# Attention with a low-rank expert layer on one core: one product tile of the first pair is moved between the two halves of block 1's values, and block 0's gates are transposed one item later

## Chip, cores and metric

One Trainium2 chip, one of its cores. The metric is the device time of one execution in microseconds (us). The kernel before was run four times: 2584.33, 2585.94, 2585.36 and 2582.39 us, median 2584.85 us.

## The reference, cut to what matters

Two sequences of 2048 rows with 2048 features each are normalised; the result feeds a single-head attention of width 512 and a low-rank expert layer with a router. Both are added to the input.

```python
xn = _layernorm(x)
x = x + attn(xn, Wqkv, bqkv, Wo, bo) + ffn(xn, A_w, B_w, Wq_w, keys)
# attn: q, k, v = xn @ Wqkv + bqkv;  softmax(q k^T / sqrt(512)) v;  @ Wo + bo
# ffn:
q      = xn @ Wq_w.T                  # 16 router features of a row
scores = q @ keys.T                   # 64 experts
gate   = softmax over the 16 largest scores, 0 elsewhere
z      = xn @ A_w.T                   # 64 experts x 8
out    = (z * gate) @ B_w.T * 2
```

Everything is float32. All products are made from a high part and a low part of each operand, so each product of two 128-wide pieces is three matmuls.

## The kernel before, in words

**Blocks and pairs.** The 4096 rows are cut into blocks of 512 rows; two blocks make a pair. The first stage (up to 1296 us) makes queries, keys, gated features and values of all blocks. The later stages (scores, softmax, weighting, output product) are not touched by the change. A pair's product is computed with seven block products in place of eight (`PHASES`: P1, P2, P6, P5, P3, P7, P4), from sums and differences of the four quarters of the input (`xq` tiles) and of the weights. The first pair is special. Its block 0 is made in the plain way (`first_block`, L319 and on, then `features`, L866), and for block 1 the values are made in two halves of the input's features, called Q and R (`values_by_half`, L902).

**Units of work ("items").** An item is what one or two loaded weight pieces feed:

- `features()`: 12 items k = 0 to 11. Each has 8 products, that is 24 matmuls with 512 columns.
- `values_by_half()`: phases Q and R, for each h = 0, 1 and g = 0, 1. One (phase, h, g) is 48 matmuls with 264 columns. The four row tiles t of one h accumulate in four PSUM banks over g = 0 and 1.
- `third()` (L948): the six P3 tiles in the order `MIXED` = 0, 2, 4, 1, 3, 5. Each is 24 matmuls with 512 columns; ScalarE copies the result into a `wu` tile (L964).
- Then `phase(0, "P6")`, P5, P7 and P4, each with six items of 24 matmuls.

**Weight pieces.** The list `pieces` (L588) fixes the order in which pieces are loaded. At the end of each item `fetch(n + 1)` (L602) issues the load of the piece two items ahead on SyncE's DMA queue (L621), casts it on ScalarE to its high part (`split_hi`, L127) and subtracts on VectorE for its low part (`split_lo`, L130). The raw tiles `pw` have three slots and the split tiles six (three pieces).

**PSUM.** `acc()` hands out seven banks in rotation. In Q and R each h takes four of them. So the last of the four tiles of (R, 1) gets the bank of the first tile of (R, 0), and a matmul into it has to wait until that tile has been read out.

**What leaves R.** `values_half_out` (L931) first adds the 16 router columns of each of the four tiles into `qr1` (L942), then calls `values_out` (L291 and on) for each: VectorE adds the Q half (L302), ScalarE casts the high part (L127), VectorE makes the low part (L130), and `store`/`flush` (L170) sends the tile to `v_d`. The tile `vs` has two slots (`mid(0, 1)`), so the third tile's add needs the first tile's store to have landed.

**Side work, dealt by hand.** `beside_F` and `beside_V` say what is recorded after which item. For the stretch in question this is: `L[n]`, `S_[n]`, `O[n]` (`part_load`, `part_sums`, `part_out`, L1160 to L1175): loads of weight quarters, four sums on GpSimd (`four_sums`, L537, lines 540 to 543) and the stores of the results to `sq_d`, from which later pieces are loaded; `b1` (`whole`, L1137) and `t2` (L666): sums on VectorE that later phases need; `p6`: splits of `t` tiles for P6; `st`: row statistics of block 2 (loads of `xs` on ScalarE's queue, L243, and `bn_stats` on VectorE, L225); and the router of block 1: `router(qr1)` (a transposition, L463), `choose` (L468: scores, the 16 largest, softmax, result `wk`), and later `gates` (L497: transposition of `wk`, L500, copy, four stores to `gd`).

**What sets the order.** A list scheduler orders the instructions of each engine before the run; `behind(...)` tells it to place a step behind some instruction already recorded. At run time every engine and every DMA queue works strictly in that order, and waits on semaphores.

**Block 0's gates.** In `features()`, after item 0 comes `router`, after item 1 `choose`, after item 3 `gates(0, wk)` (L896). The two gate tiles are loaded (`gate`, L513) at items 8 and 9, and first used on VectorE at the end of item 10 (L531).

Of the kernel before, what the change touches and what calls it, by code (L numbers as in the profile page):

```python
# [62 lines left out]
def attn_ffn_kernel(ctx: ExitStack, tc, x, xT, wq, wv, wob, bqk, bv, bo, keysT, out):  # L63
# [17 lines left out]
    def big(*js):  # L81
        return Ring(sb, *(f"B{j}" for j in js))
# [17 lines left out]
    def acc(n=None):  # L100

        if n is None:
            n = banks.pop(0)
            banks.append(n)
        return psum.tile([P, T], F32, name="acc", tag=f"acc{n}", bufs=1)

    def misc(shape=None):
        return psum.tile(shape or [P, T], F32, name="misc", tag="misc", bufs=1)
# [352 lines left out]
    def router(qr):  # L461
        pt = misc([P, P])
        nc.tensor.transpose(pt, qr.rearrange("p t r -> p (t r)"), ident)  # L463
        qT = r_qT([P, P], F32, "qT")
        nc.scalar.copy(qT, pt)
        return qT

    def choose(qT):  # L468
        psc = misc([P, NT, NE])
        nc.tensor.matmul(  # L470
            psc.rearrange("p t e -> p (t e)"), qT, kblk.rearrange("p t e -> p (t e)"),
            start=True, stop=True,
        )
        sc = r_sc([P, NT, NE], F32, "sc")
        nc.scalar.copy(sc, psc)
        wk = r_wk([P, NT, NE], F32, "wk")
        m8 = const.tile([P, NT, 2, 8], F32, name="m8")
        for t in range(NT):
            nc.vector.max(m8[:, t, 0, :], sc[:, t, :])
            nc.vector.match_replace(wk[:, t, :], m8[:, t, 0, :], sc[:, t, :], LOW)  # L480
            nc.vector.max(m8[:, t, 1, :], wk[:, t, :])
            nc.vector.match_replace(wk[:, t, :], m8[:, t, 1, :], wk[:, t, :], LOW)
        nc.vector.tensor_tensor(
            sc, sc, m8[:, :, 0, 0:1].to_broadcast([P, NT, NE]), ALU.subtract
        )
        nc.scalar.activation(sc, sc, AF.Exp)
        nc.vector.scalar_tensor_tensor(wk, wk, LOW, sc, ALU.is_equal, ALU.mult)
        sm = const.tile([P, NT], F32, name="sm")
        nc.vector.tensor_reduce(sm, wk, AX.X, ALU.add)
        nc.vector.reciprocal(sm, sm)  # L490
        nc.vector.tensor_scalar(sm, sm, 2.0, None, ALU.mult)
        nc.vector.tensor_tensor(
            wk, wk, sm.unsqueeze(2).to_broadcast([P, NT, NE]), ALU.mult
        )
        return wk
# [17 lines left out]
    def gate(gf, n):  # L513
        g = r_g([P, T], F32, "g")
        nc.sync.dma_start(g, gf[n * P : (n + 1) * P, :])
        return g
# [37 lines left out]
    def value_sums(m):  # L554
# [32 lines left out]
    MIXED = (0, 2, 4, 1, 3, 5)  # L587
    pieces = [  # L588
        (0, "F", 2 * p + f1, ch) for p in range(NFP // 2) for ch in range(2) for f1 in range(2)
    ]  # L590
    pieces += [(0, ph, h, g) for ph in "QR" for h in range(2) for g in range(2)]
    pieces += [(0, "P3", it, 0) for it in MIXED]
    pieces += [(0, ph, it, 0) for ph in ("P6", "P5", "P7", "P4") for it in range(NFP)]
    pieces += [
        (j, ph, it, g)
# [270 lines left out]
    def features():  # L866


        tiles, qT, wk, gx = {}, None, None, {}
        for k, (_, _, fp, ch) in enumerate(pieces[:12]):  # L870
            if ch == 0:
                tiles[fp] = acc()
            ps, w = tiles[fp], ready.pop(k)
            if fp >= 2 * 2 and ch == 0:
                gx[fp - 4] = gate(gfs[0], fp - 4)
            for c in range(HC):
                product(
                    ps, lambda a: w[a][:, c * P : (c + 1) * P], lambda b: xn[ch * HC + c][b],
                    c == 0 and ch == 0, c == HC - 1, ch == 1,
                )  # L880
            last["dve1"] = last["dve"]
            fetch(k + 2)
            flush()
            if ch == 0:
                if fp % 2 == 0:
                    XU[0, fp // 2] = r_xu([P, 2, T], F32, "xu")
                nc.scalar.copy(XU[0, fp // 2][:, fp % 2, :], ps)
            else:
                feature_out(0, ND * (fp // 2) + fp % 2, ps, gx)
            with behind("pe"):  # L890
                if k == 0:
                    qT = router(qr)
                if k == 1:
                    wk = choose(qT)
                if k == 3:
                    gfs[0] = gates(0, wk)  # L896
            with behind("sp", "pe", "dve1"):
                for st in beside_F.get(k, []):
                    st()
        return len(tiles) * 2  # L900

    def values_by_half(n):  # L902

        for ph in "QR":
            tiles = [tsp[0, ph, 0], tsp[0, ph, 1]]
            for h in range(2):
                ps = [acc() for t in range(NT)]
                for g in range(2):
                    w = ready.pop(n)
                    n += 1  # L910
                    for cc in range(HC // 2):
                        c = g * HC // 2 + cc
                        x_ = tsp[0, ph, c // 2]
                        for t in range(NT):
                            sl = slice(t * P, (t + 1) * P)
                            product(
                                ps[t][:, :VH], lambda a: x_[a][:, c % 2, sl],
                                lambda b: w[b][:, cc, :], c == 0, c == HC - 1,
                            )
                    last["dve1"] = last["dve"]  # L920
                    fetch(n + 1)
                    if g == 1:
                        flush()
                        values_half_out(ph, h, ps)
                        flush()
                    with behind("sp", "pe", "dve1"):
                        for st in beside_V.get((ph, h, g), []):
                            st()
        return n

    def values_half_out(ph, h, ps):  # L931
# [13 lines left out]
                u = XV[0][:, t, :] if h == 0 else YV[0][t // 2][:, t % 2, :]  # L945
                values_out(1, t, h, r_vs, qr1, ps[t][:, :VH], u)

    def third(n):  # L948

        r_w = big(25), big(27), big(28)  # L950
        for m, it in enumerate(MIXED):
            ps, w = acc(), ready.pop(n)
            n += 1
            for c in range(HC):
                product(
                    ps, lambda a: w[a][:, c * P : (c + 1) * P],
                    lambda b: tsp[0, "R", c // 2][b][:, c % 2, :], c == 0, c == HC - 1,
                )
            last["dve1"] = last["dve"]
            fetch(n + 1)  # L960
            flush()
            if it % 2 == 0:
                WU[it // 2] = r_w[it // 2]([P, 2, T], F32, "wu")
            nc.scalar.copy(WU[it // 2][:, it % 2, :], ps)  # L964
            with behind("sp", "pe", "dve1"):
                for st in beside_V.get(m, []):
                    st()
        return n
# [17 lines left out]
    for k in range(NKS - 1):  # L986
        g = seq.index((k, "P3"))
# [184 lines left out]
    def part_out(n):  # L1172
# [4 lines left out]
    L, S_, O = ([lambda n=n, f=f: f(n) for n in range(8)] for f in (part_load, part_sums, part_out))  # L1177
    x01, x11 = x_steps(0, 0, 1), x_steps(0, 1, 1)
    b0, b1 = raw_steps(0), raw_steps(1)
# [3 lines left out]
    t2 = sum_steps(0, nc.vector, (0, 0), (0, 0), (0, 1), ALU.add)  # L1183
    p6 = split_steps(0, "P6", 0, 0)
# [15 lines left out]
    qr1 = None  # L1200
    state = {}
# [3 lines left out]
        ("Q", 1, 0): [O[2], L[4]] + t3[2:],  # L1205
        ("Q", 1, 1): [S_[4], L[5]] + r_[:2],
        ("R", 0, 0): [O[3], S_[5]] + r_[2:],
        ("R", 0, 1): [O[4], L[6]],
        ("R", 1, 0): [O[5], L[7], S_[6], lambda: state.update(q=router(qr1))] + b1[:2],
        ("R", 1, 1): [S_[7]] + b1[2:],  # L1210
        0: [O[6], lambda: state.update(w=choose(state["q"]))] + t2[:2],
        1: [O[7]] + p6[:1] + t2[2:],
        2: p6[1:2] + st[:2],
        3: st[2:4],
        4: p6[2:] + st[4:6],
# [1 line left out]
    }  # L1217
    r_ev = big(27, 28)
    n = features()
    qr1 = const.tile([P, NT, 32], F32, name="qr1", bufs=1)  # L1220
    nc.gpsimd.memset(qr1, 0.0)
    n = values_by_half(n)
    r_t = big(*T_SLOTS[4:], *T_SLOTS[:4])
    n = third(n)
    r_ev = big(27, 28, 29, 9)
    (la, sa, oa), (lb, sb_, ob), (lc, sc_, oc), (ld, sd_, od) = (value_sums(m) for m in range(4))
    one = lambda: gfs.update({1: gates(1, state["w"])})
    n = phase(0, "P6", n, {0: [la], 1: [sa, one], 3: [oa], 4: [lb]})
    n = phase(0, "P5", n, {0: [sb_], 2: [ob], 3: [lc]})
    n = phase(0, "P7", n, {0: [sc_], 2: [oc], 3: [ld]})  # L1230
    n = phase(0, "P4", n, {0: [sd_], 2: [od]})
    for j in PAIRS[1:]:
        for ph in PHASES:
# [5 lines left out]
            n = phase(j, ph, n)  # L1239
# [19 lines left out]
    S, tag_of, mbc, pt_, M, L, av, rl_, vt_, lsum = {}, {}, {}, {}, {}, {}, {}, {}, {}, {}  # L1259
# [224 lines left out]
    tw, S_, U, xo, bo_bc = {}, {}, {}, {}, {}  # L1484
# [228 lines left out]
    for j in range(1, NPAIR):  # L1713
# [3 lines left out]
        for n in range(7):  # L1717
            g = NG1 * j - (14, 7, 5, 4, 3, 2, 1)[n]
            if j > 1:
                deal(g, [loads[n], splits[n]], (5, 3)[n > 0])  # L1720
            else:
                g = (44, 49, 51, 52, 53, 54, 55)[n]
# [10 lines left out]
    for g in range(begin[-1]):  # L1733
# [6 lines left out]
        j, n = divmod(g, NG1)  # L1740
# [38 lines left out]
    while done < NW * NPAIR:  # L1779
# [3 lines left out]
        if d == 0 and 1 <= c <= 18:  # L1783

            k, part = (c - 1) // 2, (c - 1) % 2
# [13 lines left out]
    for q in range(2 * NG):  # L1799
# [4 lines left out]
        for n, step in enumerate(STEPS):  # L1804
# [17 lines left out]
            while at and at[0] <= n + 7 * q - 7 * (NG - 1):  # L1822
                at.pop(0)
                k = 14 - len(at)
# [47 lines left out]
```

## Time and profile before

| | us |
|---|---|
| median of 4 runs | 2584.85 |
| lowest and highest | 2582.39, 2585.94 |
| the profiled execution's own time | 2584.33 |
| its span, first to last instruction | 2582.5 |
| TensorE busy in the span | 2556.9 |
| VectorE, ScalarE, GpSimd busy | 1973.7, 927.7, 556.1 |

The profiled execution lies 0.52 us below the median of the runs, and 1.83 us of its time lie outside the span.

The stretch that the change touches runs from about 94 us (item 3 of `features()`) to about 262 us (the start of P5). Three windows of it give this table (busy us of each engine, DMA as the mean busy share of the DMA engines):

| window (us) | what runs | TensorE | VectorE | ScalarE | GpSimd | DMA |
|---|---|---|---|---|---|---|
| 94 to 140 | features, items 4 to 11 | 44.13 of 46 | 40.30 | 16.32 | 19.68 | 0.88 |
| 140 to 194 | Q and R | 49.47 of 54 | 49.88 | 16.81 | 46.56 | 0.85 |
| 194 to 262 | P3 and P6 | 68.00 of 68 | 53.44 | 28.51 | 15.35 | 0.87 |

How to read the views: the list of waits says which engine and line waited for which, and for how long; the timeline lists instructions in order of time, merged when equal ones follow each other, with the idle time before them and what ended it in square brackets. `SPq` and `ACTq` are the DMA-issuing instructions of SyncE's and ScalarE's queues.

### The profile page before, as it was taken

Reading aid. Unit: us, or ns where it says so; the run is one execution under the profiler, and the core shown is the slowest. Engines: PE = TensorE matmul, PEld = TensorE weight load, DVE = VectorE, ACT = ScalarE, POOL = GpSimd, SP = SyncE. Lnnn points to the kernel's source line nnn. Section 1 sums busy time; section 2 is a strip of 40 time slices with the busy share of each in tenths; the row PEclk is TensorE's granted clock in tenths of the full one; section 3 lists DMA queues with packets and bytes.
Section 4 is the critical chain, followed back from the end, with each engine's and each line's share of the span. In section 5 each row is a group of like instructions: output and inputs, shape, how many; then the busy total and the mean of one; then the engine's idle time right before and its main releaser. Section 6 shows DMA issues by size and latency. Waiting matters only on the chain. (4 is left out here: it accounts for less than half of the span.)

```text
span 2582.5 us, 34226 instructions
## 1 busy us (share of the span) xinstructions
PE 2556.9 (99%) x12546; PEld 2161.2 (84%) x12546; DVE 1973.7 (76%) x2692; ACT 927.7 (36%) x1327; POOL 556.1 (22%) x340
## 2 busy tenths in 40 slices
PE   8999999999999999999999999999999999999999
PEld 7888888888888889888887888888878888888887
DVE  7797997867777678776768779688597676797675
ACT  4333333233332323343345446354364222332221
POOL 2382310001000000000100000000013665576654
PEclk9999999999999999999999999999999999999999
DMA  8988964668356673677898798898897544665552
GB/s 291 307 293 288 354 223 144 224 214 277 128 177 224 208 251 124 199 267 265 309 329 303 240 340 282 281 326 289 276 313 272 178 161 154 203 203 179 167 169 100
DMA packets 334297, 615.41 MB, mean 238 GB/s; under 512 B 28409, under 2 KB 151345, under 8 KB 334129
## 3 DMA queue, kind: packets, MB, share of 16 engines
q1 hardware_dynamic: 318864, 583.33, 66.1%
q10 hardware_dynamic: 15264, 29.89, 3.4%
q8 instruction: 99, 1.62, 0.3%
q14 instruction: 70, 0.57, 0.1%
HBM read 457.76 MB, written 155.35 MB: 237 GB/s over the span
## 5 line engine op out<-in xcount | busy, mean ns | idle before, releaser
L135 PE MATMUL acc<-t,pw 128*128 128x512 f32 x3744 | 858.0, 390 | 0.2 <-DVE t L130 0.2
L135 PEld LDWEIGHTS acc<-t,pw 128*128 128x128 f32 x3744 | 700.2, 188 | 145.9 <-DVE t L130 0.6
L1619 PE MATMUL acc<-wb,s 128*128 128x512 f32 x2688 | 609.4, 389 | 0.0
L1619 PEld LDWEIGHTS acc<-wb,s 128*128 128x128 f32 x2688 | 504.5, 188 | 104.8
L1603 POOL TENSOR_TENSOR xo<-xo,bo_bc 128x512 f32<-128x512 f32 x128 | 215.4, 1691 | 884.1 <-DMA bo_bc<-in_bo 588.9
L127 ACT CAST pw<-pw 128x1024 fp32r<-128x1024 f32 (+1 forms) x218 | 230.2, 1058 | 428.5 <-PE acc L135 286.3
L135 PE MATMUL acc<-ph,vt 128*128 128x512 f32 x1536 | 378.3, 391 | 1.3 <-ACT ot L1464 0.9
L130 DVE TENSOR_TENSOR pw<-pw 128x1024 fp32r<-128x1024 f32 (+1 forms) x218 | 288.2, 1322 | 88.2 <-ACT pw L127 88.1
L135 PEld LDWEIGHTS acc<-ph,vt 128*128 128x128 f32 x1536 | 288.4, 188 | 64.0 <-issue 2.2
L1325 PE MATMUL acc<-qt,kt 128*128 128x512 f32 x1344 | 333.9, 390 | 2.8 <-ACT sp L1335 1.5
L135 PE MATMUL acc<-pw,t 128*128 128x264 f32 x2400 | 295.4, 284 | 5.9 <-DVE vs L302 4.5
L135 PEld LDWEIGHTS acc<-pw,t 128*128 128x128 f32 x2400 | 294.1, 189 | 8.0 <-issue 4.7
L1325 PEld LDWEIGHTS acc<-qt,kt 128*128 128x128 f32 x1344 | 251.5, 188 | 58.4 <-ACT sp L1335 1.9
L127 ACT CAST s<-xz 128x1024 fp32r<-128x1024 f32 x112 | 118.0, 1055 | 374.1 <-PE acc L1619 310.5
L130 DVE TENSOR_TENSOR s<-xz,s 128x1024 fp32r<-128x1024 f32 x112 | 169.0, 1511 | 43.0 <-ACT s L127 43.0
L130 DVE TENSOR_TENSOR t<-xq,t 128x1024 fp32r<-128x1024 f32 x108 | 140.9, 1312 | 23.1 <-ACT t L127 23.0
L534 POOL TENSOR_TENSOR zt<-zt,g 128x512 f32<-128x512 f32 x28 | 45.0, 1615 | 518.1 <-DMA g<-gd 202.9
L127 ACT CAST t<-xq 128x1024 fp32r<-128x1024 f32 x108 | 113.1, 1051 | 111.7 <-DVE xq L666 52.5
L1608 DVE TENSOR_TENSOR xo<-xo,acc 128x512 f32<-128x512 f32 x128 | 87.0, 681 | 58.2 <-POOL xo L1649 30.1
L127 ACT CAST ph<-sp 128x512 fp32r<-128x512 f32 x128 | 79.4, 620 | 117.9 <-PE acc L135 117.0
L225 DVE BATCH_NORM_STATS2 st<-xs 128x6 f32<-128x512 f32 x128 | 85.0, 683 | 41.4 <-DMA xs<-in_x 41.1
L1335 ACT COPY sp<-acc 128x512 f32<-128x512 f32 x128 | 74.8, 585 | 109.6 <-PE acc L1325 109.3
(174 smaller groups left out, 2262.8 us busy)
## 6 DMA issues: line engine op xcount, KB each, us to landing
vt<-v_d SPq DMA_DIRECT2D x128, 512.0 KB, 5.4
kt<-kp_d SPq DMA_DIRECT2D x224, 256.0 KB, 5.8
pw<-sq_d SPq DMA_DIRECT2D x96, 512.0 KB, 4.2
pw<-in_wq SPq DMA_DIRECT2D x72, 512.0 KB, 3.7
xo<-in_x SPq DMA_DIRECT2D x128, 256.0 KB, 3.1
xz<-oz_d SPq DMA_DIRECT2D x64, 512.0 KB, 4.4
out_y<-xo SPq DMA_DIRECT2D x128, 256.0 KB, 2.6
xq<-in_xT SPq DMA_DIRECT2D x56, 512.0 KB, 4.7
```

The costliest lines, as they stand in the source:

```text
L127: return nc.scalar.copy(hi, src)
L130: return (eng or nc.vector).tensor_tensor(lo, src, raw(hi), ALU.subtract)
L135: last["pe"] = nc.tensor.matmul(ps, st(a_), mv(b_), start=first and n == 0, stop=end and n == 2, skip_group_check=more,)
L225: nc.vector.bn_stats(st[:, parts, :], xt[:, h * 512 : (h + 1) * 512])
L534: nc.gpsimd.tensor_tensor(zt, zt, gx[n], ALU.mult)
L1325: last["pe"] = nc.tensor.matmul(ps, st[:, d, a, :], mv[c][:, d, :], start=not more and d == 0 and i == 0, stop=d == 1 and i == 2, skip_gro ...
L1335: last["copy"] = nc.scalar.copy(*ops)
L1603: nc.gpsimd.tensor_tensor(xs, xs, bo_bc[q // (NB // 2 * NH), c], ALU.add)
L1608: nc.vector.tensor_tensor(xs, xs, ps, op)
L1619: nc.tensor.matmul(ps, st[a_][:, kk, sl], mv[b_], start=not more and kk == 0 and n == 0, stop=kk == ND - 1 and n == 2, skip_group_check=more,)
```

## The change

The order of the pieces, of the items and of the side work changes in one place; the arithmetic does not.

- P3's first tile (`MIXED[0]`) is multiplied after (R, 0) and before (R, 1). `pieces` is reordered accordingly, `values_by_half` calls `third(n, 0)` behind (R, 0), and `third` takes the numbers of the tiles that it is to make.
- `gates(0, wk)` is called after item 4 of `features()` and not after item 3.
- The side work between (R, 0, 1) and the P3 tile 1 is dealt anew: `O[5]` moves one place ahead, `L[7]`, `S_[6]`, `router` and the first of `b1` to the moved P3 tile, `t2` ahead into (R, 1), `choose` behind P3's second tile.

```diff
     ]
-    pieces += [(0, ph, h, g) for ph in "QR" for h in range(2) for g in range(2)]
-    pieces += [(0, "P3", it, 0) for it in MIXED]
+    pieces += [(0, ph, h, g) for ph, h in (("Q", 0), ("Q", 1), ("R", 0)) for g in range(2)]
+    pieces += [(0, "P3", 0, 0), (0, "R", 1, 0), (0, "R", 1, 1)]
+    pieces += [(0, "P3", it, 0) for it in MIXED[1:]]
...
                 if k == 1:
                     wk = choose(qT)
-                if k == 3:
+                if k == 4:
                     gfs[0] = gates(0, wk)
...
                         for st in beside_V.get((ph, h, g), []):
                             st()
+                if ph == "R" and h == 0:
+                    n = third(n, 0)
         return n
...
-    def third(n):
-
-        r_w = big(25), big(27), big(28)
-        for m, it in enumerate(MIXED):
+    r_w = big(25), big(27), big(28)
+
+    def third(n, *ms):
+
+        for m in ms:
+            it = MIXED[m]
             ps, w = acc(), ready.pop(n)
...
         ("R", 0, 0): [O[3], S_[5]] + r_[2:],
-        ("R", 0, 1): [O[4], L[6]],
-        ("R", 1, 0): [O[5], L[7], S_[6], lambda: state.update(q=router(qr1))] + b1[:2],
-        ("R", 1, 1): [S_[7]] + b1[2:],
-        0: [O[6], lambda: state.update(w=choose(state["q"]))] + t2[:2],
-        1: [O[7]] + p6[:1] + t2[2:],
+        ("R", 0, 1): [O[4], L[6], O[5]],
+        0: [L[7], S_[6], lambda: state.update(q=router(qr1))] + b1[:2],
+        ("R", 1, 0): [S_[7]] + b1[2:] + t2[:2],
+        ("R", 1, 1): [O[6]] + t2[2:],
+        1: [O[7], lambda: state.update(w=choose(state["q"]))] + p6[:1],
         2: p6[1:2] + st[:2],
...
-    n = third(n)
+    n = third(n, 1, 2, 3, 4, 5)
```

## The prediction

> **What bounds the kernel now.** I read the page's first two lines, then the list of TensorE's waits, then the timelines of the engines around the two waits that the change aims at.
>
> ```profile
> span 2582.5 us, 34226 instructions
> PE 2556.9 (99%) x12546; PEld 2161.2 (84%) x12546; DVE 1973.7 (76%) x2692; ACT 927.7 (36%) x1327; POOL 556.1 (22%) x340
> ```
>
> TensorE is busy in 2556.9 of 2582.5 us. The change removes no matmul, so the 25.6 us of idle time are all that any reordering can win. Who owns them (line, releaser, total, times, longest):
>
> ```profile
> PE acc L135 <- DVE vs L302: 4.5, 1, 4.5
> ...
> PE misc L500 <- DVE wk L492: 1.9, 1, 1.9
> ...
> PE acc L135 <- DVE t L130: 0.2, 1, 0.2
> ```
>
> The first is the PSUM wait at (R, 1), the second the wait for block 0's gates. Together 6.4 us, 0.25% of the time: the ceiling of the gain. TensorE's own timeline (start, length, group, idle before it) places them:
>
> ```profile
> 96.43 0.41 PE L500 MATMUL misc<-ident,wk 128*128 128x128 f32 x2 [1.86 <-DVE wk L492]
> ...
> 140.25 36.05 PE L135 MATMUL acc<-pw,t 128*128 128x264 f32 x297
> 180.83 6.45 PE L135 MATMUL acc<-pw,t 128*128 128x264 f32 x39 [4.53 <-DVE vs L302]
> 187.11 0.27 PE L463 MATMUL misc<-ident,qr 128*128 128x128 f32 x1
> ...
> 198.74 38.48 PE L135 MATMUL acc<-t,pw 128*128 128x512 f32 x168
> ...
> 262.33 0.96 PE L135 MATMUL acc<-t,pw 128*128 128x512 f32 x3 [0.15 <-DVE t L130]
> ```
>
> Steps from these: 36.05/297 = 0.121 us for a 264-column matmul, 38.48/168 = 0.229 for a 512-column one; so (R, h) lasts 96 x 0.121 = 11.65 us and a P3 tile 24 x 0.229 = 5.5 us. The last row matters too: at P5's start TensorE reached VectorE's work just as it was done.
>
> Why was the bank late at 180.8? VectorE's timeline:
>
> ```profile
> 127.47 4.89 DVE L1137 TENSOR_TENSOR xq<-xh 128x512 f32<-128x512 f32 x8
> ...
> 173.47 6.81 DVE L1137 TENSOR_TENSOR xq<-xh 128x512 f32<-128x512 f32 x4
> 180.20 0.16 DVE L942 TENSOR_TENSOR qr<-acc,xv 128x16 f32<-128x16 f32 x1
> 180.28 0.40 DVE L302 TENSOR_TENSOR vs<-acc,xv 128x248 f32<-128x248 f32 x1
> ...
> 181.01 0.24 DVE L942 TENSOR_TENSOR qr<-acc,xv 128x16 f32<-128x16 f32 x2
> ...
> 185.96 0.40 DVE L302 TENSOR_TENSOR vs<-acc,xv 128x248 f32<-128x248 f32 x1
> ```
>
> The reads of (R, 0)'s tiles stand behind VectorE's other work, without a gap. Four sums of line 1137 take 6.81 us here, 1.70 each, and 0.61 each at 127 us: GpSimd is at work beside these four (46.56 of 54 us in this window), and each VectorE sum pays about 1.1 us. VectorE is thus the bound of the Q and R stretch, and TensorE only shows it.
>
> **A row and a rule on this.** The Trainium skill, "SBUF — State Buffer", section "Who interferes with whom", says that VectorE and GpSimd share one port pair as an exclusive lock, the loser waiting for the other's whole instruction. By that a VectorE operation would pay up to a GpSimd operation's own 1.3 us where the rows show 1.1; step 5's 3.3 below would be 3.9, against the change.
>
> **Part by part, in the clock of the trace of before.**
>
> 1. *Gates an item later.* The transposition moves 24 matmuls back, to 94.6 + 5.5 = 100.1; `wk` was ready at 96.3, so the 1.9 us wait goes. Its consumers: the gate tiles were loaded at 106.8 and first used at 135.7, so 5.5 us later is hidden by 20 us. In the changed order the four `gd` stores (3.3 us of issuing) stand in front of two weight loads, which issued at 106.5 and 110.6 before: no cost. If they did meet, the cost is at most those 3.3 us. TensorE is then 1.9 us ahead, less up to 0.9: the last `t` tile of R was split at 171.28 and needed at 172.3, a margin of 1.0.
>
> 2. *P3's tile between the halves.* (R, 0) ends near 175.2; the tile needs weights and `t` tiles that are split by 171.3, and lasts to 180.7, or 178.8 with the gates' gain. Its copy to `wu` on ScalarE needs `O[5]` to have left the buffer (the last of its stores was issued by 176.7): free. (R, 1) then takes the first two banks of (R, 0) for its third and fourth tile, read out by 181.1.
>
> 3. *A wait that takes its place.* In the changed order the router's transposition (line 463) stands directly behind the P3 tile and ahead of (R, 1), not inside it as at 187.11. It needs all four `qr1` adds, the last done at 181.25. So TensorE starts (R, 1) at about 181.4, however early it came: the gates' 1.9 us are lost here, and 0.7 to 2.6 us of wait are new. (R, 1) ends at 181.4 + 11.7 = 193.1. Before, it ended at 193.0 with six P3 tiles to go; now five. If nothing else waits, the gain is 5.5 us at this point.
>
> 4. *Weights of (R, 1, 1).* SyncE's queue before:
>
> ```profile
> 170.30 0.38 SPq L621 DMA_DIRECT2D pw<-sq_d  x1
> 170.77 5.97 SPq L1175 DMA_DIRECT2D sq_d<-hs  x4
> 176.79 1.45 SPq L1166 DMA_DIRECT2D hs<-in_wq  x3
> 181.71 0.53 SPq L170 DMA_DIRECT2D v_d<-vs  x1
> ```
>
> In the changed order the four `sq_d` stores (`O[5]`, held up by GpSimd until 176.4) come ahead of this load. It is issued at 176.8 and lands 5.0 to 7.9 us later (the medians of the two kinds of `pw` load in 140 to 215 us), cast and split take 2.3 to 3.4: ready at 184.1 to 188.1, needed at 181.4 + 5.8 = 187.2. Cost 0 to 0.9; I take 0.
>
> 5. *Weights of P3's second tile.* They are needed at 193.1. In the changed order VectorE does the third tile's add (line 302) first, straight after the first two low parts. That add needs the first `vs` store landed: issued 181.71, landing in 2.6, so 184.3. Before, other work filled that time and the add came at 185.96. Now VectorE is idle from about 182 to 184.3, and behind it stand, by their spacing without GpSimd: two adds 0.7, weights of (R, 1, 1) 1.2, two low parts 0.7, four sums of line 1137 2.4, two of line 666 2.3, then these weights 1.2: 8.4 us, so 192.7 at the earliest. But the loads `L[7]`, issued from 176.79 before, now stand behind two `vs` stores (182.2), so GpSimd's last four sums (`S_[7]`) start at 187.3, not 185.85, right beside the sums of 1137 and 666. They cost 0 to 4 times 1.1: split at 192.7 to 197.1. I take three meetings, 196.0. TensorE waits 2.9 us (0 to 4.0) and starts P3's second tile at 196.0, where it was 198.74: 2.7 us ahead.
>
> 6. *The chain behind it.* From 196.0 VectorE has two sums, two splits and the adds of (R, 1) (to 201.2), a weight split and two low parts (to 203.1). Their `v_d` stores now stand behind a weight load that waits for that split; with landings of 3.5 to 5.4 us the third add of (R, 1) comes near 207, then its cast on ScalarE, and behind it ScalarE's queue holds the first three `xs` loads of block 2's row statistics. These were issued at 205.8 to 206.8 before; now at 207 to 208, about 1 us later, although TensorE is earlier. From 212 to 262 VectorE waits for `xs` for 0.2, 1.8, 3.8, 2.8 and 1.9 us: this chain of loads sets its pace, and at 262.33 TensorE had no slack against it. If the chain holds, TensorE stops at P5 at the latest, 1 us later than before; if those 10.5 us of idle time absorb it, the 2.7 us remain. I take +0.5, nearer to the row at 262.33.
>
> Behind P6 the queues hold the same order as before, so a shift passes to the end as it is.
>
> **Sum.** -1.9 (gates) -4.5 (bank) +0.9 (transposition, net of step 2) +2.9 (second tile's weights) + 3.1 (chain at P6 and P5) = +0.5. The profiled execution took 2584.3; that gives 2584.8, and as the median of the runs is 0.5 above it, I say **2585.0 us**: no change that a measurement of this kernel can tell (0.2% is 5.2 us, about that limit).
>
> **Rivals.**
>
> - *The gain stays.* GpSimd does not meet VectorE in step 5 (192.7), and the statistics chain follows TensorE: 2584.3 - 5.5 = 2578.8. For it: three of VectorE's rows at 184.15 ran at 0.63 each while GpSimd paused. Against it: `S_[7]` must fall into that list, and the row at 262.33. Chance 0.16.
> - *VectorE's queue locks up, slower.* Mechanism: the third add waits for a `vs` store with all weight splits behind it, twice, in (R, 0) and (R, 1). Price: the upper ends, weights of (R, 1, 1) at 188.1 (+0.9, and the list of step 5 late by 2), P3's second tile at 199, the second add at 210, `xs` loads 4 us late, and one more weight split each for P3's later tiles: about +6, 2590.3. It decides when the first `xs` load is issued later than 211. Chance 0.22.
> - *The change does not do what it says:* the bank wait survives on the two banks that (R, 1) still shares. They are read by 181.1, before step 3 lets TensorE go; so this is inside the forecast.
>
> **Numbers.** Forecast (within 0.2%) 0.62, gain stays 0.16, queue locks up 0.22. The unknown costs of steps 3 to 6 span -5.5 to +6, from the first rival's time to the second's; the range takes them in: 2578.8 to 2590.3. Beyond it lie a gain without any new wait and a second lock-up in P6, under 2 in 10 together. Faster by over 0.2% 0.16, within 0.62, slower 0.22.
>
> **What would show it.** The profile after should have no wait on line 302 near 180 and none on L492; a wait of TensorE on `qr` at the transposition; one of about 3 us on `pw` (line 130) 11.7 us later; VectorE idle about 2 us before its third add of line 302, released by the store; `xs` loads from about 207. I am wrong if P3's second tile starts by 194, or if P5 starts clearly before 262.

## The result and the profile after

The changed kernel is slower by a little: median 2589.78 us against 2584.86 us of the kernel before beside it, ratio 1.0016, 95% interval 1.0012 to 1.0021, that is 3.1 to 5.4 us. This straddles the 0.2% (5.2 us) named in the prediction and hardly leaves it; but the sum had come to +0.5, and this is about +4. The profiled execution of the changed kernel took 2593.39 us (span 2591.6), 3.6 more than its median and more than each of the 40 other runs (highest 2593.12), so the readings below are taken from one stretch, up to 290 us, and totals from the ratios. The ratios are not the quotients of the medians and differ from them by up to 0.09%. One of the twelve runs of the tile alone (2819.23 us) was in the slow state and is left out of its ratio.

The page's first lines, then the list of TensorE's waits (line, releaser, total, times, longest), of the changed kernel:

```profile
span 2591.6 us, 34226 instructions
...
PE 2558.7 (99%) x12546; PEld 2160.4 (83%) x12546; DVE 1978.2 (76%) x2692; ACT 928.3 (36%) x1327; POOL 557.3 (22%) x340
```

```profile
PE acc L135 <- DVE pw L130: 6.3, 3, 5.2
...
PE acc L135 <- DVE t L130: 3.1, 3, 1.9
...
PE misc L463 <- DVE qr L945: 1.4, 1, 1.4
```

The two waits that the change aims at (4.5 on L302, 1.9 on L492) are gone from this list. In their place stand one of 5.2 us on a weight split, one of 1.4 on the router columns, and more for `t` tiles. TensorE's timeline of the changed kernel places them (start, length, group, idle before it):

```profile
99.77 0.38 PE L500 MATMUL misc<-ident,wk 128*128 128x128 f32 x2
...
174.64 5.62 PE L135 MATMUL acc<-t,pw 128*128 128x512 f32 x24
181.66 0.33 PE L463 MATMUL misc<-ident,qr 128*128 128x128 f32 x1 [1.40 <-DVE qr L945]
...
199.56 7.63 PE L135 MATMUL acc<-t,pw 128*128 128x512 f32 x24 [5.15 <-DVE pw L130]
...
234.30 1.66 PE L135 MATMUL acc<-t,pw 128*128 128x512 f32 x6 [1.93 <-DVE t L130]
...
287.47 0.27 PE L264 MATMUL misc<-ident,mr 128*8 128x128 f32 x1
```

The last row in the kernel before:

```profile
281.27 0.27 PE L264 MATMUL misc<-ident,mr 128*8 128x128 f32 x1
```

The second row is the moved P3 tile. The fourth is P3's second tile, predicted at 196.0: it starts at 199.56, and its 24 matmuls take 7.63 us where the first tile's take 5.62. From there TensorE is behind the kernel before: the transposition of line 500 in P6 starts at 243.27 (237.06 before), the one at P5's end (L264) at 287.47 (281.27 before). So 6.2 us of the 9.1 between the two profiled executions arise in this stretch. The other 2.9 come later, where VectorE, ScalarE, GpSimd and SyncE have the same orders in both kernels, and stay unexplained.

Why 199.56? VectorE's timeline of the changed kernel:

```profile
181.52 0.83 DVE L130 TENSOR_TENSOR vs<-vs 128x248 fp32r<-128x248 f32 x2
186.80 0.42 DVE L302 TENSOR_TENSOR vs<-acc,xv 128x248 f32<-128x248 f32 x1 [4.45 <-DMA v_d<-vs]
187.13 1.25 DVE L130 TENSOR_TENSOR pw<-pw 128x1056 fp32r<-128x1056 f32 x1
...
192.78 4.52 DVE L667 TENSOR_TENSOR xq<-xq 128x1024 f32<-128x1024 f32 x2
197.22 2.28 DVE L130 TENSOR_TENSOR pw<-pw 128x1024 fp32r<-128x1024 f32 x1
...
210.66 0.43 DVE L302 TENSOR_TENSOR vs<-acc,yv 128x264 f32<-128x264 f32 x1 [2.15 <-DMA v_d<-vs]
```

The third add of line 302 stands still for 4.45 us until the first `vs` store has landed, and the split of the weights of (R, 1, 1) stands right behind it. The same happens again at 210.66 in (R, 1). SyncE's queue gives the other half:

```profile
182.05 1.20 SPq L170 DMA_DIRECT2D v_d<-vs  x2
183.30 3.72 SPq L1171 DMA_DIRECT2D hs<-in_wq  x4
```

The store is issued at 182.05, and VectorE goes on at 186.80: 4.7 us. All four loads of `L[7]` now stand behind it; in the kernel before three of them were issued at 176.79.

### The profile page after: what moved, and what is told of

Read it like the earlier page. It is cut to its first block, busy times and chain, and to the rows that moved or that the text cites. A ratio compares the mean times of both kernels' runs of the same rounds, so it can differ in the third digit from the quotient of the medians.

```text
span 2591.6 us, 34226 instructions
## 1 busy us (share of the span) xinstructions
PE 2558.7 (99%) x12546; PEld 2160.4 (83%) x12546; DVE 1978.2 (76%) x2692; ACT 928.3 (36%) x1327; POOL 557.3 (22%) x340
## 5 line engine op out<-in xcount | busy, mean ns | idle before, releaser
L1608 POOL TENSOR_TENSOR xo<-xo,bo_bc 128x512 f32<-128x512 f32 x128 | 209.3, 1643 | 891.4 <-DMA bo_bc<-in_bo 592.3
```

Of the source, the lines that this page charges most:

```text
L1608: nc.gpsimd.tensor_tensor(xs, xs, bo_bc[q // (NB // 2 * NH), c], ALU.add)
```

## The experiments

Theory 1 at the start: the loss comes from VectorE's queue, where the third add waits for a store with the weight splits behind it. Rivals: GpSimd's last sums beside VectorE's (2), the gates' move (3). The clock (theory 4, rival 6) and the interplay of the two moves (rival 5) came in as results asked for them. Each ratio is to runs of the kernel before on the same chip, with its 95% interval. The expected times start from 2584.9 us; on these chips the kernel before had medians of 2585.3 to 2586.3.

**The gates alone.**

```diff
-                if k == 3:
+                if k == 4:
                     gfs[0] = gates(0, wk)
```

> The kernel before with the gates' move alone. Before 2584.9, after 2589.8. Theory 1 (the loss is made by the moved tile, in VectorE's queue behind it: the store wait of line 302 and what stands behind it): the gates' move by itself costs nothing and takes the 1.9 us wait on wk away, but as VectorE is the bound at (R, 1) the bank wait then grows by what TensorE is earlier; 2583.0 to 2584.9, no slower than before. Rival 3 (the gates' later stores and tiles make the loss): 2588 to 2590.

Measured: 2586.49 us, ratio 0.9997 (0.9988 to 1.0006). No loss and no gain, and the time lies between the two expected: rival 3 falls for the gates by themselves. In its trace the wait on line 492 is gone, but the bank wait on line 302 has grown from 4.53 to 5.16 us.

**The tile alone.** The change without that line.

> The changed kernel with the gates where they were before: the tile's move alone. Theory 1: the wait on wk is back (1.9 us), but TensorE waits for the qr1 adds at the transposition less by the same, so the time is the changed kernel's, 2588.5 to 2591. Rival 3 (the gates make the loss): 2583 to 2586.

Measured: 2586.84 us, ratio 0.9997 (0.9986 to 1.0008). This lies in neither expected range: no part alone shows a cost, both together cost 0.16%. Its trace shows what differs. The scheduler has put the third add of line 302 behind the split of the weights of (R, 1, 1) and two sums, and three of the loads `L[7]` are issued at 179.19, ahead of the `vs` stores. VectorE waits 0.48 us for stores in all, and P3's second tile starts after a wait of 0.40 us. So the order in two queues, which the diff does not show, differs between the change and its tile alone.

**A third slot for `vs`.**

```diff
     n = features()
+    r_vs = Ring(sb, "h0", "h1", "B26")
...
+    r_vs = mid(0, 1)
     r_ev = big(27, 28, 29, 9)
```

> The changed kernel with a third slot in the ring of vs tiles while block 1's values are made, so that the third add of line 302 no longer waits for the landing of the first store. Theory 1 (the store wait is the head of the loss): the 4.45 us wait at 182.4 to 186.8 and the 2.15 us one near 210 go, P3's second tile starts about 4 us earlier, at 195 to 196, TensorE's wait in front of it shrinks from 5.15 to 1 or 2 us and the half clock behind it goes too (2 us): 2583.5 to 2586. Rival 2 (GpSimd's S_[7] beside the sums makes the loss): VectorE reaches those sums earlier but GpSimd, held by its load until 190.7, still meets the last ones: 2588 to 2590.

Measured: 2588.21 us, ratio 1.0009 (1.0000 to 1.0018): by its middle about half of the loss, though the interval reaches from none to all of it, and the time missed theory 1's range and lies in rival 2's. The third add no longer waits, but the fourth does, 1.29 us, and it too stands ahead of the split. P3's second tile starts at 197.39 after 3.34 us.

**GpSimd's last sums later.**

```diff
-        0: [L[7], S_[6], ...
-        ("R", 1, 0): [S_[7]] + b1[2:] + t2[:2],
-        ("R", 1, 1): [O[6]] + t2[2:],
+        0: [S_[6], ...
+        ("R", 1, 0): b1[2:] + t2[:2],
+        ("R", 1, 1): [O[6], L[7]] + t2[2:],
```

`S_[7]` and `O[7]` go to P3's second and third tile.

> The changed kernel with the last portion of the Q sums (its load L[7], GpSimd's sums S_[7] and their stores) dealt one or two items later, so that GpSimd is idle while VectorE makes the sums in front of the weights of P3's second tile. Rival 2 (the meetings with GpSimd make the loss): each of about three to four sums is 1.1 us shorter and the loads that stood beside the first vs store are gone: P3's second tile at 195 to 196 and 2584 to 2586. Theory 1 (the store wait makes it): the 4.45 us wait stays unless the store lands earlier with less traffic beside it, the tile starts at 197 to 199 and the time is 2587 to 2590; if the store lands in 2.6 us instead of 4.7, 2 us less of that.

Measured: 2590.49 us, ratio 1.0021 (1.0012 to 1.0030). Rival 2 falls, in an instructive way. TensorE's timeline of this kernel:

```profile
193.80 5.62 PE L135 MATMUL acc<-t,pw 128*128 128x512 f32 x24
...
214.81 16.72 PE L135 MATMUL acc<-t,pw 128*128 128x512 f32 x61 [4.03 <-DVE pw L130]
```

P3's second tile starts without a wait, almost 6 us earlier than in the changed kernel, and 21 us later TensorE gives back 4.03 us for another weight split. The store waits are still there (4.12 and 1.92 us), though `L[7]` no longer stands beside the first store.

**The adds later, first try.** The last two adds of (R, 0) were placed behind a sum of line 1142.

```diff
+                    with behind("whole"):
+                        for t in range(2, NT):
+                            values_out(1, t, h, r_vs, qr1, ...)
```

> The changed kernel with one order changed by hand on VectorE: the third and fourth add of line 302 of (R, 0) stand behind the split of the weights of (R, 1, 1) and the first two sums behind it, as they stood in the kernel with the tile's move alone; gates and tile are moved as in the change. Theory 1, narrowed (the loss is the order in which the scheduler put the third add: ahead of that weight split, so that the store wait holds the split, and by it the slot that the load of P3's next weights needs): no wait of 4 us on line 302, P3's second tile from about 195, no half clock there, 2584 to 2586.5. Rival 5 (the two moves together cost by something else, such as TensorE being earlier or the gates' stores, and that order is only another symptom): 2588.5 to 2590.5.

Measured: 2591.03 us, ratio 1.0019 (1.0009 to 1.0029). The edit named a sum that stands ahead of the adds anyway, so VectorE's order stayed that of the changed kernel: this is a repeat of it, and tells nothing of the order. As a repeat it shows how much one execution differs from another. Its store waits are 2.76 and 2.64 us, and TensorE's timeline reads:

```profile
196.44 7.33 PE L135 MATMUL acc<-t,pw 128*128 128x512 f32 x24 [3.22 <-DVE pw L130]
...
231.90 11.04 PE L135 MATMUL acc<-t,pw 128*128 128x512 f32 x35 [2.93 <-DVE t L130]
```

P3's second tile starts 3.1 us earlier than in the first profile, and yet P5's last transposition comes at 286.56, 5.3 us behind the kernel before. More of this loss arises at a `t` tile near 232: the wait of 2.93 us, and 35 matmuls in 11.04 us, where they take about 8 at full clock (35 times 0.229).

**The reverse: the tile alone, with the split held behind the third add.**

```diff
-            last["dve"] = split_lo(lo, ws, hi)
+        with behind(*["v3"] * (pieces[n] == (0, "R", 1, 1))):
+            last["dve"] = split_lo(lo, ws, hi)
```

> The reverse: the tile's move alone (gates as in the kernel before), with the split of the weights of (R, 1, 1) held on VectorE behind the third add of line 302, as in the changed kernel. Theory 1, narrowed: a store wait of 3 to 5 us appears in VectorE's queue near 185 to 188, TensorE waits 3 us or more for P3's second tile, and the time goes from 2586.8 up to 2588.5 to 2591. Rival 5: the order is no cause, 2585 to 2587.

Measured: 2590.97 us, ratio 1.0023 (1.0014 to 1.0032), against 0.9997 (0.9986 to 1.0008) without this line: the intervals are apart. So VectorE's order makes a loss of this size, with the gates where they were. It is not the add alone: with that line the scheduler also put three sums (one of `b1`, two of `t2`) behind the split of the weights of P3's second tile. SyncE's order stayed, but for one swap near 204 us. VectorE's timeline of this kernel shows both waits:

```profile
185.98 0.42 DVE L302 TENSOR_TENSOR vs<-acc,xv 128x248 f32<-128x248 f32 x1 [2.73 <-DMA v_d<-vs]
...
210.53 0.43 DVE L302 TENSOR_TENSOR vs<-acc,yv 128x264 f32<-128x264 f32 x1 [2.50 <-DMA v_d<-vs]
```

TensorE's wait for P3's second tile is 2.21 us, less than expected, and the tile starts at 195.80, as in the tile alone (195.64). The larger loss comes later: 2.88 us on a weight split at 215.78 (0.85 at 213.59 in the tile alone).

**The first try of the adds, with three slots.** The two edits above together.

> The kernel of the order changed by hand with three slots for vs besides, so that neither (R, 0) nor (R, 1) waits for a store of line 302. Theory 1, narrowed: the gain that the tile and the gates make, up to 5.5 us at (R, 1), now meets only the chain of row statistics at P5 (needed at 262.3 before); as the xs loads come by the casts of the third and fourth part of (R, 1), which no longer wait, P5 is reached 0 to 3 us earlier: 2582 to 2585. Rival 5: 2587 to 2590.

Measured: 2586.91 us, ratio 1.0008 (1.0000 to 1.0017), in neither expected range. As the first try left VectorE's order alone, this repeats the third slot (1.0009), and its one store wait is again 1.29 us.

**Filling TensorE's gap, in the kernel before.**

```diff
+                        if ph == "R" and h == 0:
+                            d = misc()
+                            for k in range(18):
+                                nc.tensor.matmul(d, x_[0][:, 1, :P], x_[0][:, 1, :], ...)
```

> The kernel before with 18 matmuls of 512 columns more, on data that is there anyway and into a bank that nobody reads, placed in the 4.8 us gap of TensorE at 176.0 to 180.8 in front of (R, 1): it tells what the half clock behind the gap costs. Theory 4 (an idle TensorE is what brings the half clock): the 264-column matmuls behind the gap are 0.12 us apart from the first, not 0.22, (R, 1) lasts 1.6 us less, P3 starts 1.6 us earlier, and the time is 2583.2 to 2584.9 if nothing behind it waits. Rival 6 (these matmuls are slow by the bank reads or transfers beside them): still 0.22 apart to 184, and 2584.9 or a little above.

Measured: 2588.49 us, ratio 1.0007 (0.9999 to 1.0016). The clock question is answered by busy time and granted clock in short windows (after the colon: length, then busy time and count of PE, PEld, DVE, ACT, POOL; PEclk; DMA share; GB/s). The kernel before, behind its gap of 4.8 us:

```profile
180.80:182.00 1.20, 1.17 (x5) 1.20 (x6) 0.88 (x4) 1.20 (x3) 1.12 (x2) 0.50 0.09 34
182.00:184.00 2.00, 2.00 (x11) 2.00 (x10) 1.90 (x2) 0.36 (x2) 0.82 (x1) 0.50 0.51 159
```

The same with the gap filled:

```profile
180.20:181.20 1.00, 1.00 (x10) 1.00 (x8) 1.00 (x2) 0.00 (x0) 1.00 (x1) 1.00 1.01 332
```

And the changed kernel behind its gap of 5.4 us:

```profile
199.50:201.50 2.00, 1.94 (x5) 1.57 (x6) 2.00 (x3) 0.41 (x1) 0.00 (x0) 0.50 1.05 399
201.50:203.50 2.00, 2.00 (x6) 1.61 (x5) 2.00 (x3) 0.64 (x1) 0.00 (x0) 0.50 0.87 342
```

Behind these idle stretches TensorE runs at half clock; with the gap filled it does not, though the DMA share is then higher. On the clock theory 4 holds and rival 6 falls. The filled kernel has the price too, as it runs the same 39 matmuls at clock 1.00:

```profile
182.55 4.96 PE L135 MATMUL acc<-pw,t 128*128 128x264 f32 x39 [1.11 <-DVE vs L302]
```

In the kernel before they take 6.45 us, so the half clock costs 1.5; in the changed kernel P3's second tile takes 7.63 and the first 5.62, so 2.0. The expected gain in time missed (2583.2 to 2584.9 was said). TensorE reached a bank that VectorE had not read yet (the 1.11 us above), and P3 starts at 193.27, no earlier than in the kernel before (193.03). The extra matmuls also changed VectorE's order: the last two adds of (R, 1) now stand ahead of a sum and wait 2.37 us for a store at 204.28, where the kernel before has no such wait, and TensorE loses 1.95 us on a weight split at 212.2.

**The adds really later.** The change, with the last two adds of (R, 0) recorded at (R, 1, 0), behind the sums there.

```diff
+                    if (ph, h, g) == ("R", 1, 0):
+                        with behind("whole"):
+                            for t in range(2, NT):
+                                values_out(1, t, 0, r_vs, qr1, ps0[t][:, :VH], ...)
```

> The changed kernel with the third and fourth add of line 302 of (R, 0) really moved on VectorE: behind the split of the weights of (R, 1, 1), the four sums and the first two sums of line 667. (The earlier try named a sum that already stood ahead of them, and left the order as it was.) Gates and tile as in the change. Theory 1, narrowed (the order of the third add against that split makes the loss): no store wait, the split ends near 185.5, P3's next weights are issued near 186 to 187, its second tile starts at 193.5 to 195.5 and the time is 2584 to 2587. Rival 5 (the gates' move and the tile's together cost by something else): 2588.5 to 2591.

Measured: 2589.74 us, ratio 1.0012 (1.0003 to 1.0022): the expectation of theory 1 missed, and the time lies in rival 5's range. VectorE's timeline of this kernel says why:

```profile
195.18 1.32 DVE L130 TENSOR_TENSOR pw<-pw 128x1024 fp32r<-128x1024 f32 x1 [4.21 <-ACT pw L127]
...
211.68 0.43 DVE L302 TENSOR_TENSOR vs<-acc,yv 128x264 f32<-128x264 f32 x1 [1.97 <-DMA v_d<-vs]
```

The first store wait is gone, and VectorE reaches the next weights early. But their load, issued at 187.9 right behind the four loads of `L[7]`, has landed only at 194.1. And the second store wait is still there.

**The tile alone, with three slots:** a trial for a better version.

> The tile's move alone, with the gates where they were before and three slots for vs: VectorE's order has the third add of line 302 ahead of the weight split again, but it finds a free slot, and the fourth stands behind the split. A trial for a version that beats both. Theory 1, narrowed: no store wait ahead of the split, none in (R, 1) (0.5 us in the tile's move alone), the xs loads at or before 208: 2582.5 to 2585.5. If the slots only move the wait to the fourth add, as they did in the changed kernel: 2586 to 2588.

Measured: 2583.67 us, ratio 0.9990 (0.9981 to 0.9998): ahead of both kernels, by 0.1% of the one before, just outside the interval. Its profile does not say where the gain lies: P5's last transposition starts at 282.47, 1.2 us behind the kernel before, and its span is 0.6 us shorter all the same. It is one comparison of thirteen, so I do not call this gain shown. Beside the third slot alone (1.0009, 1.0000 to 1.0018) it says something else: the two kernels differ in the gates' line only, and their intervals are apart. Their VectorE orders differ too, so the runs do not say whether the gates cost by that or in another way.

**The adds really later, and three slots.** The change with both edits.

> The changed kernel with the adds of (R, 0) really moved behind the split and the sums, and three slots for vs besides: both store waits gone. Theory 1, narrowed, with the second store wait as its second term: 2582.5 to 2585.5, P5 reached 0 to 3 us before the changed kernel with the moved adds alone. Rival 5: 2587 to 2590.

Measured: 2587.41 us, ratio 0.9999 (0.9988 to 1.0009), apart from the changed kernel's 1.0012 to 1.0021. There is no store wait in VectorE's stretch from 180 to 214 us, and by the ratio the loss is gone, with gates and tile both moved. The medians say less: 2587.41 against 2585.31 us is 0.08% more, outside the range of theory 1 and inside that of rival 5. The profiled execution, one of the longer half (2590.55), lost time without any store wait:

```profile
231.34 2.10 PE L135 MATMUL acc<-t,pw 128*128 128x512 f32 x6 [4.36 <-DVE t L130]
```

So the edit takes most of the loss out, but rival 5 is not excluded.

**One order held on SyncE:** the first two `vs` stores behind the loads `L[7]`.

```diff
+                    with behind("l7"):
+                        flush()
```

> The changed kernel, gates and tile as in the change, with one thing held: the first two vs stores of (R, 0) stand on SyncE behind the four loads L[7], not ahead of them. The scheduler then also puts the third add of line 302 behind the split of the weights of (R, 1, 1) and three sums, so both engines' queues stand nearly as in the tile's move alone, and the gates are still an item later. Theory 1 with two terms (the add ahead of the split, and the loads L[7] beside and ahead of P3's next weights): L[7] is issued near 177, the weights of P3's second tile land by 191 to 192, it starts at 193.5 to 195.5 and the time is 2583.5 to 2586.5. Rival 5 (the two moves together cost by something else, whatever the order of these queues): 2588 to 2591.

Measured: 2586.48 us, ratio 1.0007 (0.9998 to 1.0017). The scheduler now puts the third add behind the split by itself, and P3's second tile starts at 195.15, as expected. The median is at the upper end of the expectation; two short store waits remain in (R, 1), 0.30 and 1.40 us. The interval overlaps both that of the changed kernel and no change, so this run alone settles nothing.

**All of them in one table.** The third column is what VectorE waited for `vs` stores between 180 and 214 us in the profiled execution:

| kernel | ratio (95%) | store waits, us |
|---|---|---|
| adds later, three slots | 0.9999 (0.9988 to 1.0009) | 0 |
| tile alone | 0.9997 (0.9986 to 1.0008) | 0.48 |
| tile alone, three slots | 0.9990 (0.9981 to 0.9998) | 0.86 |
| gates alone | 0.9997 (0.9988 to 1.0006) | 1.02 |
| three slots; its repeat | 1.0009; 1.0008 (both about ±0.0009) | 1.29; 1.29 |
| order held on SyncE | 1.0007 (0.9998 to 1.0017) | 1.70 |
| adds later | 1.0012 (1.0003 to 1.0022) | 1.97 |
| gap filled | 1.0007 (0.9999 to 1.0016) | 2.37 |
| tile alone, add ahead | 1.0023 (1.0014 to 1.0032) | 5.23 |
| the change repeated | 1.0019 (1.0009 to 1.0029) | 5.40 |
| GpSimd's sums later | 1.0021 (1.0012 to 1.0030) | 6.04 |
| the change | 1.0016 (1.0012 to 1.0021) | 6.60 |

Kernels that wait about 1 us or less are as fast as the one before, those that wait 1.3 to 2.4 us lie between, those above 5 us take 0.16 to 0.23% more. The third column is one execution of each kernel, so this is a trend and no proof: 0.86 and 1.29 us of waits stand beside 0.9990 and 1.0009. Two edits set the wait and the time followed: one put it in (0.9997 to 1.0023), one pair took it out (1.0016 to 0.9999). That is what carries theory 1. What is shown is that VectorE's order in this stretch is worth as much as the whole loss; that the store waits alone make the 0.16% of the change is argued, and some other cost of the two moves together (rival 5) stays possible. How much each branch of theory 1 takes (the weight split behind the add, the half clock, the `xs` loads behind the second wait) the runs do not separate.

## Why the prediction was right and wrong

- **Step 1, gates: right.** The transposition starts at 99.77 (predicted 100.1) without a wait, and TensorE's lead shrinks by 0.28 and 0.57 us of waits at R (up to 0.9 was said).
- **Step 2, tile and bank wait: right.** 174.64, 5.62 us long, no bank wait. The ceiling of 6.4 us ahead of it was too low: the bank wait also cost 1.5 us of half clock, so 7.9. For the same reason the 25.6 us of idle time were not all that a reordering can win, since slow matmuls count as busy.
- **Step 3, transposition: right.** It waits 1.40 us and starts at 181.66 (said: 0.7 to 2.6, about 181.4). The gates' gain ends here, as said; in the gates alone it ends in the bank wait.
- **Step 4, weights of (R, 1, 1): right,** a wait of 0.50 (0 to 0.9).
- **Step 5, P3's second tile: too low in the profiled execution, right in the repeat.** Its words: "That add needs the first `vs` store landed: issued 181.71, landing in 2.6, so 184.3." It was issued at 182.05 and the add came at 186.80, 4.7 us later. The list behind it took 12.7 us where 8.4 + 3.3 was said: four operations' worth of meetings with GpSimd in place of three, each still at about 1.1 (the two sums of line 667 at 2.26, 1.21 where GpSimd is idle, at 199.43). TensorE waited 5.15, beyond the bound of 4.0. In the repeat the add came at 184.72, the wait was 3.22 and the tile started at 196.44, close to the 2.9 and 196.0 of the forecast; so this step alone cannot be why the sum was too low. What no term held in either is the half clock: 2.0 and 1.7 us. The 2.6 was what this very store took in the trace of before (first row, KB and median us to landing); the second row, for all of that kernel's `vs` stores, would have warned of the spread:

```profile
v_d<-vs SPq DMA_DIRECT2D x4, 248.0 KB, 2.6
...
DMA to landing us min/median/max: 2.4/4.1/7.1
```

- **Step 6, the chain: the step that failed in both executions,** right in kind, wrong in size. It was said to make TensorE 1 us later at most. The third add of (R, 1) came at 210.66 (208.56 in the repeat) and not near 207, the first `xs` load at 211.20 (209.09) and not at 207 to 208 (205.81 before). The loss showed in P3's `t` tiles near 232 (1.93 and 0.60 us; 2.93 and about 3 of half clock in the repeat), not at P5, and P5's last transposition was 6.2 and 5.3 us late.
- **The sum.** The change costs 0.16%, inside the "within 0.2%" of the forecast, but about 4 us and not 0.5: the class held by its width. The recorded 2585.0 is also not quite its own sum, 2584.8 + 0.5 = 2585.3.
- **The rival that came nearer.** "VectorE's queue locks up, slower" named two store waits with the splits behind them, P3's second tile at 199 (199.56), the second add at 210 (210.66), a first `xs` load later than 211 as the point that decides (211.20), and about +6 for +4.1 measured. It was given 0.22; the forecast of +0.5 with 0.62 was the wrong branch of the same mechanism. Part of the fit is luck: these rows are from an execution slower than all 40 others, the equally ordered repeat had 196.44, 208.56 and 209.09, and the gates alone had a first `xs` load at 211.43 without any loss, so that point decides nothing. That the two moves together would flip two queue orders was in no part of the prediction, which took the changed order as given.

## What to carry to other kernels

When a change lets one engine run ahead, look for the first ring of few slots behind it that is freed by a DMA store, and price the store's landing over the spread of its kind, not at one value. What stands behind such a wait on an in-order queue matters too: one line that held a weight split behind one add, with the sums that the scheduler moved for it, was worth 0.26% here. If a list scheduler sets the order, compare its queues for each part of a change alone and for both, since moving the gates by 24 matmuls flipped them here; and a wait removed at one tile came back 21 us later in one kernel, so the total decides, not the tile. Take more than one profile when executions of one kernel differ by as much as the effect.

## What the runs showed of the hardware

**TensorE's clock can fall after short idle stretches.** Each gap is TensorE's idle time before the group, then what 24 matmuls of 512 columns took (5.62 at full clock) or the granted clock. Gaps of 1.76, 2.21 and 2.46 us: 5.72 to 5.74; of 1.93: clock 1.00. Gaps of 1.95 and 1.99: clock 0.50 to 0.65 behind them. Gaps of 2.83, 3.22, 3.34, 3.50 and 5.15: 7.36, 7.33, 8.51, 8.56 and 7.63 us. So a gap from about 2 us on may cost 1.7 to 2.9 us more than itself. Its length alone does not decide: a gap of 3.10 at 17.4 us in the changed kernel left the clock at 1.00 behind it, one of 3.00 at the same place with the third slot left 0.50. The Trainium skill, "TensorE: Matmul & The Clock Gate", section "HAM oscillation — how this bites in real kernels", warns of idle gaps over about 3.4 us. The runs agree on the effect and show it from shorter gaps on. The same page, section "What's actually happening", says that the clock's window is free-running and does not start with the kernel, which would let equal gaps come out differently, as 1.95 and 2.21 did; no run here shows the window itself.

**The same store does not always land equally fast.** The first `vs` store of (R, 0) held the add for 2.76 us in one execution of the changed order and for 4.45 in another, though the order was the same. Without the loads of `L[7]` behind it the wait was 4.12 us, so these loads do not explain it.
